# Summing the states of a selective scan: identity matmuls against PE transposes that add into one PSUM group

## The chip, the core and the metric

The kernel runs on one core of a Trainium2 chip. A core has TensorE (PE, matmuls, with its weight loads shown apart as PEld), VectorE (DVE), ScalarE (ACT), GpSimd (POOL) and SyncE (SP, which here issues transfers). PE writes its results to PSUM, and DVE and ACT read them from there; POOL works on the other memory, SBUF, alone. The metric is the device time of one execution in microseconds (us), the median of several runs, of the kernel before and the kernel after on the same chip.

## The reference

The program is four layers of a sequence model, each an attention-like block and a feed-forward block, on 2048 tokens of width 128 (8 sequences of 256 tokens in the layer that is changed). What is changed is the selective state space scan of the second layer, here cut to what matters. There are 256 inner channels and 16 states for each of them:

```python
xz = x @ W_in                                   # 128 -> 512
x_inner, z = jnp.split(xz, 2, axis=-1)
xc = silu(causal_conv4(x_inner) + conv_b)
x_ssm = xc @ W_xproj                            # 1 + 16 + 16 columns: delta, B, C
delta = softplus(delta_raw * w_dt + b_dt)
dA  = exp(delta[..., None] * A)                 # A = -exp(A_log)
dBx = delta[..., None] * Bm[:, :, None, :] * xc[..., None]
def step(h, (dA_t, dBx_t, c_t)):
    h = dA_t * h + dBx_t
    y = einsum('bdn,bn->bd', h, c_t)            # sum over the 16 states
y = y + xc * D_param
y = y * silu(z)
return y @ W_out                                # 256 -> 128
```

## The kernel before

All activations lie by channel: 128 channels on the partitions, tokens along the free dimension. A sequence of 256 tokens with 256 inner channels is a tile `[128, 2, 256]` (two halves `c` of the channels).

The stage that is touched is `local_mamba`. It interleaves three streams of work. `one_sequence` takes a sequence through two layers of local attention with their feed-forward blocks, up to four sequences at a time. Behind it `then` starts `mamba_sequence`, the state space of that sequence, with up to two of these under way. Beside the last one run loads of later weights, products of weight matrices (`fold`) and the routing of the first mixture of experts (`route1`).

In `mamba_sequence` (line 1216) the steps are: `xin` and the convolution into `xc`; `z` and `sz = silu(z)`, by channel (line 1242); `xps`, whose 33 rows go to memory and come back spread over all partitions as `bc`, with B and C of two states in each tile; `raw`, and from it `d` (delta) and `u = d * xc`. Then a loop over eight pairs of states, `m`:

- ACT makes `da = exp(d * A)`, four instructions of 128x255 (line 1295);
- DVE makes `hs = u * B` (line 1297), scans `hs` with `da` (line 1299), and multiplies by C (line 1300), each over 128x1024 elements: two states, two halves of channels, 256 tokens;
- PE adds the two states into the one PSUM tile `y` by two matmuls of 128x512 with the identity as weights (helper `mm`, line 863). Over the eight pairs 16 such matmuls form one PSUM group. In the profile an fp32 matmul is two instructions, so `y` has 256 of them for 128 matmuls.

After the loop DVE adds `xc * D_param` to `y` (line 1306, one instruction for each half), the product with `sz` follows on POOL (on DVE for the last sequence, line 1307), and `wout` takes the result to 128 channels. The residual `s` (line 1312), a layernorm and the router's logits close the sequence.

`route1` then works out for 14 of the 16 token tiles, and later for the last two, where each token goes (`put`, line 1512). `scatter` (line 1616) sends each tile of 128 tokens to its places by one indirect transfer that POOL issues, 16 in all. The first mixture of experts (`moe1`) reads `places` after all 16.

PSUM banks of the stage are shared by tag: two for the short-lived tiles (`M`: `xin`, `z`, `xps`, `raw`, `ln`, `wout` and others), two `Q`, one `A`, one `B`, one `Y` for `y`.

The order of instructions on each engine isn't the order of the program text. A planner (`_Order`) takes all instructions with their dependences, gives each a rank, its place in the text plus a correction from the table `BIAS` (by engine, tile name and stage), and a length from the table `LENGTHS`, plays the program through, and fixes the order that comes out for every engine. `STAY` is how much earlier in rank an instruction must be for PE or ACT to leave its present group (PE's shape of weights, ACT's function table). A change of these tables moves instructions in all stages.

Of the kernel before, what the change touches and what calls it, by code (L numbers as in the profile page):

```python
# [23 lines left out]
P = 128  # L24
# [285 lines left out]
class _Order:  # L310
# [12 lines left out]
    STAY = dict(PE=70, ACT=310)  # L323
    BIAS = {
        "ACT  1": 495, "ACT  3": -495, "ACT d 2": -1445, "ACT e 4": -700, "ACT e 6": 370, "ACT fh 4": -30, "ACT four 4": 630, "ACT four 5": -345,
        "ACT ge 2": 385, "ACT got 3": 50, "ACT got 5": 590, "ACT k 2": -275, "ACT kp 4": -40, "ACT lakq 2": -75, "ACT lavp 2": -95, "ACT lg 2": 620,
        "ACT lnrs 1": 225, "ACT lnrs 2": -280, "ACT lnsq 2": 40, "ACT ot 6": 75, "ACT ptsb 2": -740, "ACT qsq 2": -5, "ACT r 2": -70, "ACT rg 1": -590,
        "ACT rg 2": -320, "ACT rn 2": 55, "ACT rs 4": -50, "ACT rs 6": -25, "ACT s 6": -190, "ACT savp 2": -5, "ACT sg 3": 560, "ACT sh 5": -250,
        "ACT spl 1": -410, "ACT spt 1": -15, "ACT st 6": 460, "ACT v 2": 25, "ACT xc 2": -2725, "ACT xchunked 2": -400, "ACT xchunked 4": -390,
        "ACT xs 2": 10, "ACT xsq 4": -660, "DVE ab 4": 720, "DVE bt 3": -1225, "DVE bt 5": 190, "DVE centre 0": -205, "DVE d 2": -10,  # L330
        "DVE decaypart 4": -240, "DVE e 2": 50, "DVE four 5": 105, "DVE fs 4": 10, "DVE gate 2": -345, "DVE gate 5": -320, "DVE get 2": 180, "DVE get 4": 5,
        "DVE get 5": 850, "DVE got 4": -40, "DVE h 2": 5, "DVE h 5": -525, "DVE hs 2": 5, "DVE k 5": -680, "DVE lares 2": -200, "DVE lg 4": 665,
        "DVE nm 2": -135, "DVE nm 6": -95, "DVE oh 2": -285, "DVE oh 4": 2440, "DVE oh 5": -180, "DVE ptsb 2": 20, "DVE ptsb 6": -250, "DVE put 2": 190,
        "DVE put 4": 480, "DVE q 5": 470, "DVE q 6": 785, "DVE r 2": -120, "DVE rc 2": -270, "DVE rc 4": 175, "DVE route 2": -345, "DVE s 2": 20,
        "DVE s 5": -95, "DVE s 6": 1585, "DVE sares 2": 30, "DVE sel 4": -50, "DVE sg 3": -250, "DVE sm 4": 365, "DVE spt 1": 810, "DVE st 6": 150,
        "DVE sum 2": -705, "DVE t 5": 400, "DVE th 4": 650, "DVE u 2": 255, "DVE vec 2": 50, "DVE we 4": -30, "DVE wlocal 2": 1325, "DVE xc 2": -1830,
        "DVE xla 4": -580, "DVE xlf 4": 75, "DVE xlocal 2": -860, "DVE xmoe 6": 10, "DVE xpf 4": -10, "DVE xrglru 2": 205, "DVE xsa 4": 485, "DVE ys 3": 100,
        "DVE z 4": -190, "PE a 2": 50, "PE acc 5": 10, "PE b 2": 30, "PE bt 3": 1010, "PE bt 5": -580, "PE cum 2": 80, "PE cum 4": -1270, "PE fold 2": 105,
        "PE g 2": -700, "PE gate 1": -345, "PE gate 2": 345, "PE hps 4": -15, "PE kps 4": 95, "PE lg 2": 205, "PE lin 6": -1140, "PE ln 1": 355,
        "PE ln 2": -45, "PE o 6": -910, "PE out 4": -35, "PE pg 5": -20, "PE proj 5": 100, "PE proj 6": -570, "PE ps 4": -455, "PE pt 2": -25,  # L340
        "PE pt 4": -125, "PE pu 3": 2550, "PE pu 5": -720, "PE py 3": 740, "PE qkt 2": -1425, "PE raw 2": -1360, "PE rows 2": 585, "PE sc 2": -60,
        "PE sc 4": 30, "PE sc 6": -1215, "PE v 5": 470, "PE v 6": -20, "PE vps 2": 1025, "PE vps 4": -10, "PE wo 2": 60, "PE wo 6": -855, "PE wout 2": -95,
        "PE xps 2": -790, "PE y 2": 20, "PE z 2": 40, "PE zt 4": -20, "POOL biasrows 3": -595, "POOL e 4": 415, "POOL e 6": -305, "POOL got 5": 490,
        "POOL km 5": 665, "POOL mean 0": 635, "POOL one 0": 395, "POOL places 2": -70, "POOL places 5": -240, "POOL q 5": 50, "POOL q 6": -325,
        "POOL rest 4": -990, "POOL rg 1": -25, "POOL rows 4": 85, "POOL ss 2": -20, "POOL t 2": 595, "POOL u 2": 110, "POOL zero 0": -35,
        "POOL zeros 1": -385, "SP bc 2": 200, "SP cst 3": -455, "SP got 3": 535, "SP got 5": 505, "SP outdram 6": 275, "SP places 1": 1460,
        "SP rottable 0": 45, "SP routetables 0": 495, "SP rows 4": -370, "SP scales 2": 40, "SP vec 0": -1475, "SP wattn 2": 15, "SP wmoe 2": -150,
        "SP wmoe 4": -150, "SP wmoe 5": -100, "SP xs 2": -660,
    }
    LENGTHS = {  # L350
        "ACT  LoadActFuncSet  ": (1178, 1283), "ACT d Ln 128x512 128x512": (544, 649), "ACT da Exp 128x255 128x255": (403, 508),
        "ACT e Abs 128x256 128x256": (460, 565), "ACT e Exp 128x128 128x128": (422, 527), "ACT e Exp 128x256 128x256": (460, 565),
        "ACT e Exp 128x512 128x512": (526, 631), "ACT four Exp 128x2 128x2": (98, 203), "ACT got DMACopy 128x512 128x512": (451, 3502),
        "ACT h TensorCopy 64x255 64x255": (295, 400), "ACT k TensorCopy 128x512 128x512": (484, 589), "ACT lnrs Exp 128x256 128x256": (317, 422),
        "ACT lnsq Square 128x256 128x256": (278, 383), "ACT ot TensorCopy 128x512 128x512": (490, 595), "ACT qsq Square 128x512 128x512": (498, 603),
        "ACT r Relu 128x256 128x256": (462, 567), "ACT rg Exp 128x1020 128x1020": (1039, 1144), "ACT rg Ln 128x1024 128x1024": (949, 1054),
        "ACT rn Exp 128x16 128x16": (111, 216), "ACT rn Ln 128x16 128x16": (116, 221), "ACT rs Exp 128x2 128x2": (97, 202),
        "ACT rs Ln 128x2 128x2": (98, 203), "ACT sh Silu 128x512 128x512": (492, 597), "ACT xc Identity 128x256 128x256": (465, 570),
        "ACT xc Silu 128x512 128x512": (524, 629), "ACT xchunked TensorCopy 128x256 128x256": (260, 365), "ACT xmoe Identity 128x256 128x256": (404, 509),
        "ACT xs TensorCopy 33x256 33x256": (255, 360), "ACT xsq Square 128x128 128x128": (296, 401), "DVE biaspart TensorCopy 96x256 96x256": (198, 283),  # L360
        "DVE decay TensorScalarPtr 128x512 128x512": (516, 601), "DVE decaypart TensorCopy 128x512 128x512": (334, 419),
        "DVE four TensorScalarPtr 128x4 128x4": (74, 159), "DVE ge TensorScalarPtr 128x256 128x256": (384, 469),
        "DVE ge TensorScalarPtr 85x256 85x256": (368, 453), "DVE h TensorTensor 128x256 128x256": (317, 402),
        "DVE hs TensorScalarPtr 128x1024 128x1024": (2191, 2276), "DVE hs TensorTensor 128x1024 128x1024": (1123, 1208),
        "DVE mv BNStatsAggregate 128x2 128x6": (85, 170), "DVE nm TensorTensor 128x8 128x8": (67, 152), "DVE ptsb TensorCopy 128x512 128x512": (594, 679),
        "DVE rc Reciprocal 128x16 128x16": (158, 243), "DVE rc Reciprocal 128x4 128x4": (83, 168), "DVE rc Reciprocal 128x8 128x8": (109, 194),
        "DVE rg TensorScalarPtr 128x256 128x256": (580, 664), "DVE rottable TensorScalarPtr 128x256 128x256": (260, 345),
        "DVE s TensorScalarPtr 128x128 128x128": (253, 338), "DVE s TensorTensor 128x256 128x256": (324, 409), "DVE st BNStats 128x6 128x128": (197, 282),
        "DVE sum TensorReduce 128x32 128x448": (736, 821), "DVE t TensorScalarPtr 128x256 128x256": (385, 470),
        "DVE t TensorTensor 128x512 128x512": (595, 680), "DVE vec TensorTensor 128x1 128x1": (60, 145), "DVE vec TensorTensor 85x1 85x1": (59, 144),  # L370
        "DVE vs TensorCopy 128x512 128x512": (594, 679), "DVE wlocal TensorScalarPtr 128x682 128x682": (483, 568),
        "DVE x TensorScalarPtr 128x256 128x256": (369, 454), "DVE xc TensorScalarPtr 128x254 128x254": (384, 469),
        "DVE xla TensorScalarPtr 128x256 128x256": (429, 514), "DVE xlocal TensorTensor 128x256 128x256": (310, 395),
        "DVE xpf TensorScalarPtr 128x256 128x256": (577, 662), "DVE z TensorScalarPtr 128x128 128x128": (292, 377),
# [390 lines left out]
class _Kernel:  # L765
# [450 lines left out]
    def mamba_sequence(self, b, x, y, na, das, work, scan):  # L1216
# [22 lines left out]
        with ahead():  # L1239
            ps = self.psum("M", "z")  # L1240
            for c in range(2):
                self.mm(ps[:, c * S : (c + 1) * S], win[:, 256 + c * P : 256 + (c + 1) * P], x)
            sz = tile("sz", 2)
            nc.scalar.activation(flat(sz), ps, AF.Silu)
            self.exp_ln(nc.scalar.activation(xc, xc, AF.Silu))
# [1154 lines left out]
```

## Time and profile before

The profile is one execution; its own time stands beside the median.

| | |
|---|---|
| time, median of 3 runs | 1695.54 us (1694.59 to 1696.02) |
| time of the profiled execution | 1695.66 us |
| its span, first to last instruction | 1692.0 us |
| busy PE / DVE / ACT / POOL | 1442.4 / 1138.2 / 976.5 / 579.2 us |
| scans (line 1299), 64 instructions | 154.1 us, mean 2409 ns |
| products with B and with C (lines 1297, 1300), 64 each | 87.5 us each |
| matmuls into `y`, 256 instructions | 136.7 us, mean 647 ns |
| first and last matmul into `y` start at | 258.4 and 801.2 us |
| `D_param` step (line 1306), 16 instructions on DVE | median 471 ns |
| product with `sz` (line 1307) | 7 on POOL, median 1272 ns; 1 on DVE, 693 ns |

A busy share says how long an engine had an instruction under way. PE's instructions overlap, so the mean of one is longer than the time between two starts. An engine that is busy nearly all the time in a stretch sets its length; where none is, the idle time of the busiest and what ended it say what the others' speed is worth.

### The profile page before, as it was taken

Reading aid. Unit: us, or ns where it says so; the run is one execution under the profiler, and the core shown is the slowest. Engines: PE = TensorE matmul, PEld = TensorE weight load, DVE = VectorE, ACT = ScalarE, POOL = GpSimd, SP = SyncE. Lnnn points to the kernel's source line nnn. Section 1 sums busy time; section 2 is a strip of 40 time slices with the busy share of each in tenths; the row PEclk is TensorE's granted clock in tenths of the full one; section 3 lists DMA queues with packets and bytes.
Section 4 is the critical chain, followed back from the end, with each engine's and each line's share of the span. In section 5 each row is a group of like instructions: output and inputs, shape, how many; then the busy total and the mean of one; then the engine's idle time right before and its main releaser. Section 6 shows DMA issues by size and latency. Waiting matters only on the chain.

```text
span 1692.0 us, 28693 instructions
## 1 busy us (share of the span) xinstructions
PE 1442.4 (85%) x10858; PEld 932.5 (55%) x10858; DVE 1138.2 (67%) x2182; ACT 976.5 (58%) x2661; POOL 579.2 (34%) x535
## 2 busy tenths in 40 slices
PE   2688897979788877676679999999997998999997
PEld 1355553545454544343557776766674764566664
DVE  5755579898989898689354656566445332588885
ACT  3777887787877868644135554545443222366654
POOL 1344462616263423100331222221214004567573
PEclk7799999999999998899789999999997998999998
DMA  5000012121212213266310000000102121000000
GB/s 193 1 1 1 1 39 63 39 63 39 63 39 63 64 38 97 66 196 242 111 47 2 8 14 11 7 8 5 46 2 68 47 82 30 18 5 4 8 4 10
DMA packets 45113, 77.97 MB, mean 46 GB/s; under 512 B 5580, under 2 KB 21988, under 8 KB 43824
## 3 DMA queue, kind: packets, MB, share of 16 engines
q1 hardware_dynamic: 39648, 70.02, 13.8%
q0 software_dynamic: 3216, 5.07, 1.1%
q8 instruction: 85, 1.39, 0.3%
q10 hardware_dynamic: 2112, 1.05, 0.2%
q14 instruction: 52, 0.43, 0.1%
HBM read 66.87 MB, written 10.76 MB: 46 GB/s over the span
## 4 chain that ended last, share of the span: by engine, by line
PE 49%; DVE 23%; ACT 11%; issue 9%; POOL 5%; DMA 2%; another core or an unknown queue 0%; SPq 0%; ACTq 0%; DVEq 0%; POOLq 0%
PE vps L863 7%; PE kps L863 6%; PE sc L863 5%; PE out L863 4%; DVE hs L1299 3%; DVE hs L1300 3%; PE pu L863 3%; PE pg L863 3%; PE pt L974 3%; DVE hs L1297 2%; PE o L863 2%; ACT e L1146 2%; PE hps L863 2%; PE py L863 2%; PE acc L863 2%
## 5 line engine op out<-in xcount | busy, mean ns | idle before, releaser
L863 PE MATMUL y<-hs,ident 128*128 128x512 f32 x256 | 136.7, 647 | 30.2 <-DVE hs L1300 29.9
L1151 POOL TENSOR_TENSOR e<-e,rc 128x1024 f32<-128x1024 f32 x32 | 79.6, 2486 | 228.3 <-DVE rc L1150 227.6
L1299 DVE TENSOR_TENSOR_SCAN hs<-da,hs 128x1024 f32<-128x1024 f32 x64 | 154.1, 2409 | 0.1
L2250 ACT ACTIVATE e<-sc,nm 128x128 f32<-128x128 f32 (+1 forms) x256 | 105.1, 426 | 64.1 <-DVE nm L2245 55.2
L974 PE MATMUL pt<-ident,e 128*128 128x128 f32 x768 | 119.2, 281 | 18.0 <-POOL e L1151 12.4
L1295 ACT ACTIVATE da<-d,na 128x255 f32<-128x255 f32 x256 | 110.5, 508 | 22.5 <-DVE hs L1299 20.2
L1146 ACT ACTIVATE e<-sc,nm,rn 128x128 f32<-128x128 f32 x256 | 114.7, 468 | 10.9 <-DVE nm L1141 10.5
L974 PEld LDWEIGHTS pt<-ident,e 128*128 128x128 f32 x768 | 88.4, 143 | 56.3 <-issue 19.2
L2253 POOL TENSOR_TENSOR e<-e,rc 128x1024 f32<-128x1024 f32 x48 | 91.1, 1897 | 65.6 <-DVE rc L2252 65.5
L1829 POOL TENSOR_TENSOR e<-e,rc 128x512 f32<-128x512 f32 x32 | 33.9, 1059 | 226.1 <-DVE rc L1828 173.4
L1098 POOL TENSOR_TENSOR t<-t,t 128x512 f32<-128x512 f32 x64 | 84.1, 1316 | 61.1 <-DVE t L1085 56.0
L1651 POOL DMA_INDIRECT got<-ybuf,get x48 | 45.7, 952 | 169.0 <-DMA ybuf<-ys 87.6
L1804 ACT COPY kp<-kps 128x512 f32<-128x512 f32 x128 | 74.8, 585 | 48.5 <-PE kps L863 46.7
L1297 DVE TENSOR_TENSOR hs<-u,bc 128x1024 f32<-128x1024 f32 x64 | 87.5, 1384 | 6.2 <-POOL u L1284 5.5
L863 PEld LDWEIGHTS y<-hs,ident 128*128 128x128 f32 x256 | 47.5, 204 | 77.9 <-DVE hs L1300 47.5
L1300 DVE TENSOR_TENSOR hs<-hs,bc 128x1024 f32<-128x1024 f32 x64 | 87.5, 1369 | 0.0
L863 PE MATMUL qk<-w_local,h 128*128 128x512 f32 x128 | 71.1, 644 | 13.0 <-DVE t L1085 6.2
L976 DVE COPY ptsb<-pt 128x512 f32<-128x512 f32 x104 | 69.0, 677 | 17.0 <-PE pt L974 16.0
L1840 ACT COPY vs<-vps 128x512 f32<-128x512 f32 x64 | 37.4, 584 | 67.5 <-PE vps L863 56.8
L863 PE MATMUL vps<-sa_vp,x_lf 128*32 128x512 f32 x512 | 69.8, 594 | 0.0
L976 ACT COPY ptsb<-pt 128x512 f32<-128x512 f32 x88 | 51.4, 584 | 31.3 <-PE pt L974 30.7
L2245 DVE TENSOR_REDUCE nm<-sc 128x4 f32<-128x1024 f32 (+1 forms) x48 | 58.3, 1215 | 15.2 <-PE sc L863 14.6
(380 smaller groups left out, 3800.0 us busy)
## 6 DMA issues: line engine op xcount, KB each, us to landing
bc<-xs SPq DMA_DIRECT2D x128, 256.0 KB
w_moe<-in_e_dram SPq DMA_DIRECT2D x16, 768.0 KB
w_attn<-in_w_dram SPq DMA_DIRECT2D x4, 1024.0 KB
w_local<-in_w_dram SPq DMA_DIRECT2D x2, 1557.0 KB
places<-zeros SPq DMA_DIRECT2D x2, 1280.0 KB
got<-places SPq DMA_DIRECT2D x6, 256.0 KB
ybuf<-ys SPq DMA_DIRECT2D x8, 160.0 KB
x_in<-in_x_dram SPq DMA_DIRECT2D x1, 1024.0 KB
```

The source lines that it names most:

```text
L863: return self.nc.tensor.matmul(out, lhsT, rhs, start=start, stop=stop)
L974: self.last = self.nc.tensor.transpose(pt[:, j * P : (j + 1) * P], src[:, j * P : (j + 1) * P], self.ident)
L976: copy(sb.rearrange("p a b -> p (a b)"), pt)
L1098: nc.gpsimd.tensor_add(t1, t1, t2)
L1146: nc.scalar.activation(e[:, j, g, :], scs[:, j, g, :], AF.Exp, bias=nm[:, j, g : g + 1], scale=rq[:, j, g : g + 1], accum_out=sm[:, j, g : ...
L1151: nc.gpsimd.tensor_tensor(e, e, rc.unsqueeze(3).to_broadcast([P, 2, 4, P]), ALU.mult)
L1295: nc.scalar.activation(da[:, n, c, 1:S], d[:, c, 1:S], AF.Exp, scale=na[:, i : i + 1])
L1297: nc.vector.tensor_tensor(hs, u.unsqueeze(1).to_broadcast(shp), bn, ALU.mult)
L1299: nc.vector.tensor_tensor_scan(line(hs), line(da), line(hs), 0.0, ALU.mult, ALU.add)
L1300: nc.vector.tensor_tensor(hs, hs, cn, ALU.mult)
L2250: nc.scalar.activation(e[:, i, :], sc[:, i, :], AF.Exp, bias=nm[:, i : i + 1], accum_out=sm[:, i : i + 1])
L2253: nc.gpsimd.tensor_tensor(e, e, rc.unsqueeze(2).to_broadcast([P, n, keys]), ALU.mult)
```

## The change

The sum over states is made in the other layout, by token. For each state, four PE transposes of 128x128 (two halves of channels, two tiles of 128 tokens) write to the PSUM tile `y`, now `[128 tokens, 2 tiles, 256 channels]`, and add into one PSUM group: 8 transposes for each pair of states in place of 2 matmuls of 128x512. The data is now the weights, and the identity is the moving operand. `xc * D_param` is made beforehand, on POOL, in place in `xc`, and joins the same group by four more transposes. `sz` is made by token too (the operands of the `z` matmul change sides; 2 matmuls of 128x256 as before). One DVE product of 128x512 gates `y` by `sz`; four transposes into a PSUM tile `yg` of the `M` banks and one ACT copy of 128x512 bring the result back to channels for `wout`.

With it come new tables for the planner: `STAY`, all of `BIAS`, and most of `LENGTHS` are replaced (three lines of each stand below).

```diff
-    STAY = dict(PE=70, ACT=310)
+    STAY = dict(PE=110, ACT=480)
     BIAS = {
-        "ACT  1": 495, "ACT  3": -495, "ACT d 2": -1445, "ACT e 4": -700, "ACT e 6": 370, "ACT fh 4": -30, "ACT four 4": 630, "ACT four 5": -345,
...
+        "ACT  1": 600, "ACT bt 5": 610, "ACT da 2": -25, "ACT e 2": 5, "ACT e 4": 5, "ACT fh 4": -15, "ACT four 4": -50, "ACT four 5": 80, "ACT ge 2": 385,
...
     LENGTHS = {
-        "PE xps Matmult 33x256 128x256": (447, 602), "PE y Matmult 128x512 128x512": (1107, 1218), "PE z Matmult 128x256 128x256": (438, 599),
...
@@ mamba_sequence
-            for c in range(2):
-                self.mm(ps[:, c * S : (c + 1) * S], win[:, 256 + c * P : 256 + (c + 1) * P], x)
+            for t in range(2):
+                self.mm(ps[:, t * S : (t + 1) * S], x[:, t * P : (t + 1) * P], win[:, 256:512])
...
             eng.tensor_mul(u, d, xc)
+            nc.gpsimd.tensor_tensor(xc, xc, self.v("dpar", 0, 2).unsqueeze(2).to_broadcast([P, 2, S]), ALU.mult)
         yield 3.0
-        yp = self.psum("Y", "y")
+        yp = self.psum("Y", "y").rearrange("p (t c d) -> p t c d", t=2, c=2)
+
+        def gathered(src, first, last):
+            for c in range(2):
+                for t in range(2):
+                    self.nc.tensor.matmul(
+                        yp[:, t, c, :], src[:, c, t * P : (t + 1) * P], self.ident, start=first and c + t == 0, stop=last and c + t == 2, is_transpose=True
+                    )
+
...
             for n in range(2):
-                self.mm(yp, self.ident, flat(hs[:, n]), m == 0 and n == 0, m == 7 and n == 1)
+                gathered(hs[:, n], m == 0 and n == 0, False)
             yield 2.3
-        yg = tile("t")
+        gathered(xc, False, True)
+        nc.vector.tensor_tensor(flat(sz), yp.rearrange("p t c d -> p (t c d)"), flat(sz), ALU.mult)
+        ps = self.psum("M", "yg")
         for c in range(2):
-            nc.vector.scalar_tensor_tensor(yg[:, c, :], xc[:, c, :], self.v("dpar", c), yp[:, c * S : (c + 1) * S], ALU.mult, ALU.add)
-        eng.tensor_mul(yg, yg, sz)
+            for t in range(2):
+                nc.tensor.transpose(ps[:, c * S + t * P : c * S + (t + 1) * P], sz[:, t, c * P : (c + 1) * P], self.ident)
+        nc.scalar.copy(flat(sz), ps)
         ps = self.psum("M", "wout")[:, 0:S]
         for c in range(2):
-            self.mm(ps, wout[:, c, :], yg[:, c, :], c == 0, c == 1)
+            self.mm(ps, wout[:, c, :], sz[:, c, :], c == 0, c == 1)
```

In the order that the planner fixes, the sequences, the pairs of states and the layers of local attention follow each other on DVE much as before: 246 DVE instructions of other kinds stand ahead of the first product with C, where there were 247, and 604 ahead of the 61st, where there were 609. Near the end of the stage two things move. The conversion `put` for the first 14 token tiles, which stood behind the scan of the last pair of states of the last sequence, now stands ahead of the scan of its fourth pair. And the conversions and sums of the gate (`L1535` before) stand between the last pairs rather than behind them. The orders of all other stages differ in many places as well.

## The prediction, made before the changed kernel ran

> **What bounds the kernel now.** I read the busy table by stage first. The stage of the change runs from the first scan (about 240 us) to the last product (803 us):
>
> ```profile
> 240.00:803.00 563.00, 452.34 (x2474) 261.31 (x2474) 496.68 (x576) 413.11 (x1035) 197.66 (x168) 0.95 0.29 82
> 803.00:830.00 27.00, 10.10 (x43) 7.67 (x43) 7.13 (x29) 4.45 (x9) 14.44 (x17) 0.56 0.25 66
> 830.00:1300.00 470.00, 440.56 (x4801) 323.80 (x4800) 261.63 (x844) 215.61 (x509) 105.08 (x114) 0.96 0.08 22
> 1300.00:1692.00 392.00, 363.57 (x2459) 236.12 (x2458) 230.90 (x501) 172.67 (x677) 171.53 (x122) 0.97 0.09 26
> ```
>
> The columns are the stretch, its length, busy PE, PEld, DVE, ACT and POOL, PE's granted clock, transfers. In the first row DVE is busy 496.7 of 563 us (88%), PE 452.3 (80%), ACT 413.1: DVE sets the pace, and its 66 us of idle time are what others can win back. After 830 us PE is busy 93 to 94% with work that the change doesn't touch.
>
> Second, what ended DVE's idle time in that stretch (waits, engine DVE):
>
> ```profile
> DVE t L1277 <- ACT e L1275: 18.6, 6, 5.5
> DVE s L1312 <- PE wout L863: 6.8, 3, 3.8
> DVE ss L1079 <- ACT qsq L1078: 6.8, 9, 1.5
> DVE ge L1204 <- PE a L863: 4.1, 6, 2.5
> DVE x L1179 <- PE wo L863: 3.0, 3, 1.0
> DVE ptsb L976 <- PE pt L974: 2.9, 2, 2.1
> DVE t L1083 <- PE qkt L1103: 2.5, 3, 1.3
> DVE nm L1140 <- PE sc L863: 2.0, 2, 1.6
> ```
>
> Here the numbers are the total, how often, and the longest. The rows that PE ends sum to 21.3 us. The row `ss <- qsq`, 6.8 us, is PE's at one remove, since `qsq` reads `qk`. No row has a scan waiting for PE: the matmuls into `y` come behind DVE.
>
> Third, the groups of instructions and the chain of waits, for the price of the two ways of summing:
>
> ```profile
> L863 PE MATMUL y<-hs,ident 128*128 128x512 f32 x256 | 136.7, 647 | 30.2 <-DVE hs L1300 29.9
> L976 ACT COPY ptsb<-pt 128x512 f32<-128x512 f32 x88 | 51.4, 584 | 31.3 <-PE pt L974 30.7
> 292.30 1.72 PE y L863 x4
> 831.15 0.44 PE bt L1643 x4
> ```
>
> In the chain, one pair of states (four instructions into `y`) costs 1.72 us, 0.43 each. Four transposes of 128x128 cost 0.44 us, 0.11 each, with their weight loads behind them.
>
> Fourth, the timeline at the end of the stage, DVE and POOL:
>
> ```profile
> 798.45 0.14 DVE L1512 CAST put<-route 128x14 int32<-128x14 f32 x1
> 799.48 1.32 POOL L1616 DMA_INDIRECT places<-x_chunked,put  x1 [50.34 <-DVE get L1523]
> 801.11 0.99 POOL L1616 DMA_INDIRECT places<-x_chunked,put  x1 [0.30 <-issue]
> 813.43 0.18 DVE L1512 CAST put<-route 128x2 int32<-128x2 f32 x1
> 819.24 0.97 POOL L1616 DMA_INDIRECT places<-x_chunked,put  x1 [0.30 <-issue]
> 821.44 1.49 SPq L1636 DMA_DIRECT2D got<-places  x3
> ```
>
> POOL had waited 50 us for `put` of the first 14 tiles. From 799.5 to 820.2 us its 16 scatters, one each 1.28 us, are what the next stage waits for.
>
> **The change part by part.** The sum is made against the profiled execution: 1695.66 us, 0.12 us above the median.
>
> *DVE.* Removed: 16 instructions of line 1306 at 0.471 us (7.5 us) and the last sequence's own product, 0.69 us. Added: 8 gates of 128x512 with one operand in PSUM; the nearest row, line 1083 of that form, has 0.68 us: 5.4 us. DVE has 2.8 us less in a stage that it paces, and I count it whole. For the gate, the other PSUM row of this size (the copy at line 976, mean 0.677) gives the same; a row without PSUM (line 1307, 0.693) gives 2.7.
>
> *PE.* Removed: 256 instructions at 0.43 us, 110 us. Added: 512 transposes at 0.11 us, 56 us; and 8 times 8 for `xc` and the way back, 7 us. PE has 47 us less of 452. That is not on the path: `y` is only 10.7 us of the chain between 240 and 803 us, of 85 us that PE has on it. What it is worth is a shorter queue ahead of the other matmuls, so a part of 21.3 + 6.8 = 28.1 us of DVE's idle time. Lower bound 0 (those waits may all be latencies), upper bound 28.1. The saving on the chain itself gives 10.7 x 47/110 = 4.6 us directly; PE's share of the stage falls by a tenth, and a queue falls by more than its load does. I take 8 us, between the direct 4.6 and half of the bound.
>
> *The way back.* From the last product of a sequence to `wout`, before: 4 instructions into `y` and their drain (799.85 to 801.83 in the timeline), two halves of line 1306, the product with `sz`, in all 3.8 us for the last sequence. After: 12 transposes at 0.11 and one drain of 0.16 (four take 0.60 from the first start), the gate 0.68, four transposes 0.60, one ACT copy 0.58, four hand-overs of about 0.06: 3.6 us. I count 0. The other sequences lose POOL's 1.27 us product on that path and gain the copy and the transposes, again 0. ACT's 8 copies (4.7 us) are hidden by its idle time, 150 us here; queued behind them on ACT are `da` and the exponentials of local attention, and the scan waits for `da` 0.1 us in all. With that cover gone they cost 4.7 us.
>
> *POOL.* Seven products with `sz` (1.27 us) go, eight of `xc` with `D_param` come, priced by the same row: 1.3 us more, in 365 us of idle time. They stand behind `u`, and only the last four transposes of the group need them. No step waits.
>
> *z by token.* The same 2 matmuls of 128x256: 0.
>
> *The moved scatters.* `put` of 14 tiles moves from behind the last scan (798.45) to ahead of the fourth pair's scan, which in the profile starts at 778.36. The first 14 scatters then take 14 x 1.28 = 18 us from about 779 us, beside the scans. After the last `put` (813.43) only two remain: 1.0 us to POOL's start (as 798.45 to 799.48), 1.32 + 0.30 + 0.97, and 1.2 us to the transfers, 818.2 in place of 821.4 us: 3.2 us gained. What was hidden behind POOL is late next, namely the last sequence's own chain. Moved gate sums cost nothing there: before, DVE did them while PE filled `y`.
>
> *The new order elsewhere.* Nothing in the other stages is added or removed. The table loads of ACT are 72 for 74. From 830 us on PE is full, and an order can change only the 6 to 7% of its idle time. I take 0 and keep 8 us to both sides, a tenth of the idle time of the busiest engine outside the stage (PE's: 64 us before 240 us, 29 and 28 us after 830), rounded up.
>
> Sum: 2.8 + 8 + 3.2 = 14.0, **1682 us**.
>
> [...] In the profile PE's granted clock is 0.98 from 240 to 640 us, where matmuls of all kinds fill it, and 0.83 and 0.87 in these two, where it is less busy:
>
> ```profile
> 640.00:680.00 40.00, 30.41 (x140) 16.58 (x138) 37.71 (x37) 30.74 (x83) 10.69 (x7) 0.83 0.35 90
> 680.00:720.00 40.00, 25.50 (x97) 13.27 (x98) 27.25 (x31) 26.20 (x51) 6.72 (x7) 0.87 0.25 67
> ```
>
> [...]
>
> **The rivals.** *PE's relief is hidden* (DVE is full, its waits are latencies): only 2.8 + 3.2 remain, 1689.7 us. For it: no scan waits for PE. Against it: 21.3 us of idle time that PE's results end.
>
> *The hand-over gives it back.* `yg` takes one of two `M` banks and crosses to ACT, so `wout` comes later; DVE's 6.8 us at `s <- wout` double: 1689.7 + 6.8 = 1696.5 us, no change. For it: ACT is 73% busy, and its queue is in order. Against it: POOL made the same detour before.
>
> *The clock falls* (slower). Place: all of 240 to 803 us. Price: the 85 - 11 = 74 us of other PE work on the chain stretch with 0.95/clock. At 0.70, midway between 0.83 above and the 0.56 of the idle stretch after 803 us, that is 26 us, so 1682 + 26 = 1708 us. It decides from the clock at which 74 x (0.95/clock - 1) = 14, that is 0.80; the two stretches above are nearly there already. Against it: PE stays 72% busy, (452 - 47) of 563 us, and local attention's matmuls stand between the transposes until 640 us.
>
> **How the numbers follow.** My forecast 0.46; relief hidden 0.20; given back 0.11; clock 0.23. The likeliest case alone reaches from 1668 (PE's relief at two thirds of its bound, 3 us from the order elsewhere) to 1690. For 8 in 10 the range is 1664 to 1704: below, 26 of the 28.1 us of idle time instead of 8; above, a clock of 0.73 (22 us by the same formula). A measurement of this kernel tells 0.2%, 3.4 us, from no change: faster 0.66 (the first two), same 0.11, slower 0.23.
>
> **What would show it.** Right: four transposes into `y` in 0.44 us; DVE's busy time in the stage 3 us lower and its idle time 60 us or less; the last PE-ended waits shorter; two scatters alone after the last `put`; the stages from 830 us on of the same length within 4 us each. Wrong: a clock under 0.8 between 240 and 803 us; more idle time ahead of `s` at `wout`; a stage without an edit that is 8 us or more off, which would mean that the new order, and not the sum, decides.

## The result and the profile after

The changed kernel took 1706.5 us, the median of 19 runs (1694.64 to 1713.39), beside 1695.54 us for the kernel before in as many (1693.65 to 1698.13). The ratio is 1.0055, with a 95% interval of 1.0042 to 1.0068: 9 us slower (the medians differ by 11), where 14 us faster was forecast. The runs of the changed kernel spread over 19 us, those of before over 4.5. The profiled execution is one of the quicker ones: 1701.73 us, span 1699.7 us.

First the busy table by stage of the changed kernel (columns as before: stretch, length, PE, PEld, DVE, ACT, POOL, clock, transfers); the last three rows are the chunked attention, the second mixture of experts and the rest:

```profile
240.00:803.00 563.00, 431.09 (x2786) 295.57 (x2784) 498.56 (x566) 419.25 (x1047) 224.81 (x177) 0.90 0.28 79
640.00:812.00 172.00, 109.76 (x630) 81.14 (x628) 143.31 (x146) 93.82 (x213) 41.98 (x29) 0.74 0.44 144
826.40:1270.80 444.40, 425.91 (x4659) 309.85 (x4660) 237.85 (x713) 207.25 (x473) 91.15 (x100) 0.97 0.08 24
1270.80:1470.30 199.50, 179.13 (x899) 115.63 (x891) 73.55 (x239) 49.86 (x109) 51.54 (x52) 0.94 0.18 51
1470.30:1699.70 229.40, 206.08 (x1733) 137.76 (x1731) 181.93 (x397) 135.62 (x606) 134.63 (x87) 0.98 0.02 7
```

and the same three later stages in the kernel before:

```profile
821.40:1263.70 442.30, 419.50 (x4623) 310.86 (x4627) 239.31 (x710) 204.33 (x470) 91.24 (x100) 0.97 0.08 24
1263.70:1460.30 196.60, 178.06 (x933) 118.17 (x925) 72.82 (x239) 51.05 (x113) 48.62 (x50) 0.92 0.18 51
1460.30:1692.00 231.70, 211.53 (x1735) 135.66 (x1733) 181.38 (x400) 134.25 (x606) 137.53 (x89) 0.98 0.02 7
```

Against the first row before, PE has 21 us less work in the stage (452.3 to 431.1), not 47. DVE has 1.9 us more (496.7 to 498.6), not 2.8 less, and POOL 27 us more. The clock is 0.90 for 0.95, and 0.74 in the stretch after local attention, where the kernel before has 0.90 (640 to 803 us). The chunked attention, in which no instruction was edited, has 6.4 us more of PE's busy time (419.5 to 425.9), the last row 5.5 us less; over the three later rows it is 2.0 us more.

Second, what ended DVE's idle time from 240 to 805 us (total, how often, longest):

```profile
DVE t L1277 <- ACT e L1275: 11.3, 6, 3.3
DVE s L1324 <- PE wout L863: 10.2, 6, 5.7
DVE x_mamba L918 <- ACT ln_rs L917: 8.6, 3, 4.3
DVE ss L1079 <- ACT qsq L1078: 7.7, 9, 1.9
DVE ptsb L976 <- PE pt L974: 4.7, 4, 2.5
```

The wait for ACT's `e` is 7 us shorter. Of the ones that PE ends, which were to become shorter, `s` is 3.4 us and `ptsb` 1.8 us longer, and `ss`, PE's at one remove, 0.9; `ge` (4.1 to 1.0), `x <- wo` (3.0 to 0.4) and `t <- qkt` (2.5 to 1.4) did become shorter. In all PE ends 25.5 us of DVE's idle time here, for 21.7 before.

Third, the groups of the sum and of the products with B:

```profile
L1292 PE MATMUL y<-ident,hs 128*128 128x128 f32 x512 | 90.6, 323 | 41.5 <-DVE hs L1309 41.1
L1306 DVE TENSOR_TENSOR hs<-u,bc 128x1024 f32<-128x1024 f32 x64 | 94.6, 1491 | 5.6 <-POOL u L1284 4.8
```

The transposes come to 0.177 us each over the stage, where 0.11 was priced. The product with B, which is the same instruction as before, has a mean of 1491 ns in place of 1384.

Fourth, the timeline at the end of the stage, DVE, PE, POOL and SP's queue:

```profile
785.17 0.17 DVE L1524 CAST put<-route 128x14 int32<-128x14 f32 x1
786.21 2.29 POOL L1628 DMA_INDIRECT places<-x_chunked,put  x1 [19.85 <-ACT sa_vp L1756]
788.81 1.87 POOL L1628 DMA_INDIRECT places<-x_chunked,put  x1 [0.30 <-issue]
807.87 1.97 PE L1292 MATMUL y<-ident,hs 128*128 128x128 f32 x8 [1.49 <-DVE hs L1309]
822.00 0.16 DVE L1524 CAST put<-route 128x2 int32<-128x2 f32 x1
824.18 0.97 POOL L1628 DMA_INDIRECT places<-x_chunked,put  x1 [0.30 <-issue]
826.38 1.49 SPq L1648 DMA_DIRECT2D got<-places  x3
```

The scatters did move: the first 14 run beside the last pairs, and from the last `put` to the read of `places` it is 4.4 us (822.00 to 826.38) where it was 8.0. But the last `put` itself comes 8.6 us later than before (813.43), so that `got` starts 5.0 us later.

So one profile shows a stage 5 us longer and later stages 3 us longer. It can't say which of the three things in the change did it: the sum, the order inside the stage, or the order of the stages behind it. For the experiments an order was written into a kernel, instruction by instruction, for each engine; two kernels whose instructions are the same but for the sum could so be given each other's order.

One thing must be known for reading them. The runs were made in five lots. In the first two the kernel before took 1674.5 and 1674.4 us, in the other three 1695.8, 1697.1 and 1695.3. Each ratio is to the kernel before in the same lot.

### The profile page after: what moved, and what is told of

Its sections match the earlier page's. It is cut to its first block, busy times and chain, and to the rows that moved or that the text cites. A ratio compares the mean times of both kernels' runs of the same rounds, so it can differ in the third digit from the quotient of the medians.

```text
span 1699.7 us, 29309 instructions
## 1 busy us (share of the span) xinstructions
PE 1424.6 (84%) x11178; PEld 969.2 (57%) x11178; DVE 1139.9 (67%) x2173; ACT 982.0 (58%) x2667; POOL 598.4 (35%) x536
## 4 chain that ended last, share of the span: by engine, by line
PE 53%; DVE 25%; ACT 9%; issue 7%; POOL 4%; DMA 1%; another core or an unknown queue 0%; ACTq 0%; SPq 0%; DVEq 0%; POOLq 0%
PE vps L863 7%; PE kps L863 6%; PE sc L863 6%; DVE hs L1308 5%; PE out L863 4%; PE pt L974 3%; PE pu L863 3%; PE pg L863 3%; PE o L863 3%; DVE hs L1306 3%; DVE hs L1309 3%; ACT e L1146 2%; PE py L863 2%; PE hps L863 2%; PE acc L863 2%
## 5 line engine op out<-in xcount | busy, mean ns | idle before, releaser
L974 PE MATMUL pt<-ident,e 128*128 128x128 f32 x768 | 114.6, 280 | 14.5 <-POOL e L1151 6.9
L1292 PE MATMUL y<-ident,hs 128*128 128x128 f32 x512 | 90.6, 323 | 41.5 <-DVE hs L1309 41.1
L1098 POOL TENSOR_TENSOR t<-t,t 128x512 f32<-128x512 f32 x64 | 88.4, 1385 | 61.7 <-DVE t L1085 48.7
L1292 PEld LDWEIGHTS y<-ident,hs 128*128 128x128 f32 x512 | 71.5, 167 | 65.9 <-DVE hs L1309 57.6
L1306 DVE TENSOR_TENSOR hs<-u,bc 128x1024 f32<-128x1024 f32 x64 | 94.6, 1491 | 5.6 <-POOL u L1284 4.8
L1309 DVE TENSOR_TENSOR hs<-hs,bc 128x1024 f32<-128x1024 f32 x64 | 83.6, 1308 | 0.0
L863 PE MATMUL vps<-sa_vp,x_lf 128*32 128x512 f32 x512 | 78.0, 594 | 0.0
L863 PE MATMUL vps<-la_vp,x_moe 128*32 128x512 f32 x512 | 72.3, 595 | 0.6 <-DVE vs L1852 0.6
```

The lines of the kernel that those rows point to most:

```text
L863: return self.nc.tensor.matmul(out, lhsT, rhs, start=start, stop=stop)
L974: self.last = self.nc.tensor.transpose(pt[:, j * P : (j + 1) * P], src[:, j * P : (j + 1) * P], self.ident)
L1098: nc.gpsimd.tensor_add(t1, t1, t2)
L1292: self.nc.tensor.matmul(yp[:, t, c, :], src[:, c, t * P : (t + 1) * P], self.ident, start=first and c + t == 0, stop=last and c + t == 2, ...
L1306: nc.vector.tensor_tensor(hs, u.unsqueeze(1).to_broadcast(shp), bn, ALU.mult)
L1309: nc.vector.tensor_tensor(hs, hs, cn, ALU.mult)
```

## The experiments

### Transposes against matmuls of the same shape; tables exchanged (first lot)

```diff
-  yp[:, t, c, :], src[...], self.ident, ..., is_transpose=True
+  yp[:, t, c, :], src[...], self.ident, ..., is_transpose=False      # e1_mm_all
+  yp[:, t, c, :], src[...], self.ident, ..., is_transpose=b < 5      # e2_mm_late
```

> The changed kernel with the same order and layout, but the sum over states made by ordinary fp32 matmuls with the identity (data as weights) in place of transposes: about 50 us more of PE work, and work of another kind. Clock theory (transposes do not hold PE's clock up): the granted clock from 640 to 812 us, 0.74 in the changed kernel, comes back to about 0.90; the median falls to 1690 to 1699 us and the runs spread by 5 us instead of 19. Order theory (the new tables are what costs): the clock is no matter, PE is 50 us fuller, the median stays at 1705 us or rises to 1715.

> As the first, but ordinary matmuls only for the last three of the eight sequences; the first five keep transposes. Clock theory: the 6 us that the changed kernel is ahead of the one before at the fifth sequence are kept, and the loss after 570 us goes: 1686 to 1695 us, narrow spread. Order theory: 1704 to 1712 us.

Measured: 1703.22 us, ratio 1.0173 (1.0150 to 1.0196), and 1696.10 us, 1.0116 (1.0100 to 1.0132). The clock between 640 and 812 us was 0.88 and 0.84 in place of 0.74; over the whole profiled execution it was 0.945 and 0.936, for 0.930 in the changed kernel. Matmuls brought the clock back and yet no time: as ordinary fp32 matmuls these instructions kept PE busy for longer (126 us in that stretch in the first of the two, for 110), and neither kernel beats the changed one (1.0103 in the next lot, with the same time for the kernel before).

In the next two the tables alone are exchanged: `STAY`, `BIAS` and `LENGTHS` of the changed kernel in the kernel before, and the other way round.

```diff
-    STAY = dict(PE=70, ACT=310)       # e3: the kernel before; e4 the reverse
+    STAY = dict(PE=110, ACT=480)      # with all of BIAS and LENGTHS
```

> The kernel before, with the planner's tables of the changed one (order alone changes). Clock theory: 1691 to 1699 us with the narrow spread of the kernel before. Order theory: 1702 to 1708 us.

> The changed kernel with the planner's tables of the kernel before. Clock theory: a clock near 0.75 from 640 us on, a wide spread (10 us or more), 1698 to 1712 us. Order theory: 1682 to 1695 us, narrow spread.

Measured: 1740.55 us, ratio 1.0400 (1.0383 to 1.0417), and 1726.82 us, 1.0311 (1.0297 to 1.0325). None of the four times lies where one of the two theories had it; both were reckoned from a kernel before of 1695 us, which here takes 1674. With either sum the planner's tables of the other give an order that is 3 to 4% worse. This tells nothing about the sum, only that an order can weigh more than it.

### The two sums in each other's order (second lot)

```diff
-        order, _ = self.plan()
+        order = the instructions of each engine, sorted by their places in the other kernel's order
```

> The changed kernel itself, as a control on the chip of the three other runs. Both theories: 1.004 to 1.007 times the kernel before, a spread of 10 us or more, a granted clock of about 0.75 from 640 to 812 us.

> The changed kernel with every instruction that both kernels have at its place in the order of the kernel before; the new ones stand where those that they replace stood. Order theory (the new tables cost, the new sum does not): 0.988 to 0.999 of the kernel before. Clock theory (transposes let the clock sink): 1.004 to 1.015, with a clock near 0.75 from 640 us on and a wide spread.

> The kernel before with every common instruction at its place in the order of the changed kernel. Order theory: as slow as the changed kernel or slower, 1.005 to 1.02, though the clock is up (0.88 or more from 640 us on). Clock theory: 0.993 to 1.003, narrow spread.

> The kernel before, for its trace on the same chip: within 0.3% of its other runs there, the clock 0.90 from 640 to 803 us.

Measured: the changed kernel 1691.59 us, ratio 1.0103 (1.0088 to 1.0119); the new sum in before's order 1697.24, 1.0148 (1.0123 to 1.0174); **the old sum in the new order 1691.27, 1.0092 (1.0076 to 1.0108)**. The kernel before in its new order is as slow as the changed kernel, without any edit to the sum. Where that goes, by the start of `got`: the stage ends at 824.6 us (before), 825.6 (changed) and 827.7 (old sum, new order), but from there to the end it takes 849.8, 863.8 and 863.1 us. With the old order there (new sum) it is 849.4. So in this lot the order of the later stages costs 13 to 14 us with either sum.

The new sum in before's order is a miss for the order theory (0.988 to 0.999): the whole loss of 1.0148 lies in the stage, which ends at 845.4 us, 21 us later than with the old sum in that order. The new sum needs its own order in the stage, so the two don't simply add up.

What the later stages lose is for the most part PE's busy time. The sums over the three stages behind `got`, with the same 7281 PE instructions, first the kernel before, then the changed one:

```profile
sum 849.30, PE 799.74 PEld 560.06 DVE 494.10 ACT 389.10 POOL 276.57; mean PE 266.58 PEld 186.69 DVE 164.70 ACT 129.70 POOL 92.19
sum 863.80, PE 809.59 PEld 563.00 DVE 493.59 ACT 392.92 POOL 276.73; mean PE 269.86 PEld 187.67 DVE 164.53 ACT 130.97 POOL 92.24
```

Of the 14 us, 10 are PE's busy time. The groups of PE in the chunked attention, from 870 to 1250 us, again first the kernel before, then the changed one:

```profile
L863 PE MATMUL vps<-la_vp,x_moe 128*32 128x512 f32 x512 | 66.6, 594 | 0.2 <-DVE vs L1840 0.2
L863 PE MATMUL out<-vs,ptsb 128*32 128x128 f32 x912 | 37.7, 274 | 0.0
L863 PE MATMUL sc<-kp,x_lf 128*32 128x128 f32 x512 | 24.7, 275 | 0.0
```

```profile
L863 PE MATMUL vps<-la_vp,x_moe 128*32 128x512 f32 x512 | 71.7, 595 | 0.0
L863 PE MATMUL out<-vs,ptsb 128*32 128x128 f32 x908 | 43.9, 274 | 0.0
L863 PE MATMUL sc<-kp,x_lf 128*32 128x128 f32 x512 | 27.6, 275 | 0.0
```

The mean time of one instruction is the same (the profile models where a matmul ends), and so is their number, within the records that are missing; the busy time of a group is 3 to 6 us longer. Busy time counts overlapping instructions once. Counted in the two traces, the start of one `vps` follows the last by 0.094 us inside an unbroken run in both, but the 512 come in 50 runs before and in 62 in the new order; all PE instructions behind `got` come in 1280 and 1378, with either sum. So the instructions of a group overlap less with each other. That more broken runs are the reason of the 10 us fits, but was not tried by itself.

### The order of the later stages alone (third lot)

Two kernels change over at the first mixture of experts: the changed kernel with before's order from there on (e7), and the kernel before with the changed kernel's order from there on (e8).

```diff
-        order = the kernel's own
+        order = the kernel's own up to the end of the stage, the other kernel's behind it
```

> The changed kernel with its own order through the state-space stage, and from the first mixture of experts on the order of the kernel before (the instructions there are the same in both). Theory (the order of the later stages costs 14 us, whichever sum is used, and the new sum itself costs the stage 1 us): the time is that of before + 1 us, ratio 0.998 to 1.003, and from the read of the places (got) to the end it takes what before takes, within 3 us. Rival (the new sum or its low clock leaves something behind that slows the later stages): the loss after got stays, ratio 1.008 to 1.011. The reasoning on record in the prediction, that an order outside the stage changes nothing by itself, expects the same ratio as for the changed kernel, 1.010.

> The kernel before with its own order through the state-space stage, and from the first mixture of experts on the order of the changed kernel. No instruction is changed. Theory (the order of the later stages): 14 us more than before, ratio 1.007 to 1.010, all of it after got: some 10 us in the chunked attention and 5 in the second mixture of experts, with longer mean times of the 128x32-column matmuls (vps 0.130 to 0.140 us of busy time each) and not more idle time. Rival (the loss comes with the new sum): ratio 1.000. A second rival (the loss in the old-sum kernel with the new order came from the stage): also 1.000 here.

Measured: 1692.83 us, ratio **0.9979** (0.9963 to 0.9994), and 1700.28 us, **1.0036** (1.0022 to 1.0050). In the second no instruction is changed and none before `got` moved; it is slower all the same. The size is smaller than the 14 us expected: here, as in the first profile, the kernel before needs 20 us more than in the first two lots, 14 of them in the chunked attention (442.3 against 428.4 us), where the new order has less to lose. The traces of the runs with so long a kernel before say the same: from `got` to the end the three with the new order there take 873.3 to 873.6 us (the changed kernel in the first profile and in the fourth lot, and this second kernel), the nine with the old one 866.8 to 870.6. That is 3 to 7 us.

### A mixed sum (third lot)

In the changed kernel the clock was 0.95 from 240 to 640 us and 0.74 from 640 to 812, behind local attention. So sequences 0 to 4 use transposes and 5 to 7 the old sum. Of the edit the choice of the sum is shown; the other steps of the change, POOL's product among them, go with it.

```diff
+            new = b < 5
...
+                if new:
+                    gathered(hs[:, n], m == 0 and n == 0, False)
+                else:
+                    self.mm(yf, self.ident, flat(hs[:, n]), m == 0 and n == 0, m == 7 and n == 1)
```

> Sequences 0 to 4 by transposes, 5 to 7 by identity matmuls, in the changed kernel's order through the stage and in before's order from the first mixture of experts on. Theory (the transposes relieve PE while local attention fills it, and lose by the clock once it does not): the stage is 6 us ahead at sequence 4, as the changed kernel was, and then takes the 258 us from there to got that the old sum took in the new order, so got comes 3 us earlier than before: ratio 0.997 to 1.000, the granted clock from 640 us to the end of the stage 0.84 to 0.88. Rival (the loss in sequences 5 to 7 is the new order's alone): as the changed kernel's stage, ratio 1.000 to 1.003.

> As the kernel with the mixed sum, but the order goes over from the changed kernel's to before's gradually between the planner's 500 and 620 us, so that sequences 5 to 7 run in the order of before with the sum of before. Theory: 6 us ahead at sequence 4, then the 254 us that before takes from there to got: 5 to 8 us less than before, ratio 0.995 to 0.997. Rival (an order between two that were worked out for other programs fits neither): 5 us or more above before, ratio over 1.003.

Measured: 1689.96 us, ratio **0.9970** (0.9959 to 0.9982), and 1706.02 us, 1.0066 (1.0045 to 1.0087). The first is as expected. The second is a miss, and the rival stood there: in the stretch where the two orders cross, it is 86 us from the start of one sequence's delta to the next one's (`t <- e`, 566.6 to 652.6 us) where it was 73 in the first (563.7 to 636.6). Here an order between two good ones was a worse one.

### The sum alone, in one order (fourth lot)

Four kernels side by side: the changed kernel (f1); the same with before's order later (f2, the same kernel as e7, which had 0.9979 in the third lot); the old sum in that second order (f3); and the mixed sum with sequence 5 by transposes as well (f4).

```diff
-            new = b < 5
+            new = b < 6      # f4
```

> The changed kernel again, so that the next three have it beside them. Ratio 1.0055 as on the first chip, or 1.010 as on the second.

> The changed kernel with before's order from the first mixture of experts on, beside the changed kernel on one chip. Theory (the later order is the largest part of the loss): 8 to 14 us less than the changed kernel, ratio to before 0.997 to 1.002. Rival (that order costs 3 to 6 us, as the profiles on the first chip say, and the rest was the difference of chips): ratio to before 1.002 to 1.005 where the changed kernel has 1.0055, and 1.007 where it has 1.010.

> The old sum in the changed kernel's order through the stage, and before's order from the first mixture of experts on: against the run with the new sum in the same order everywhere it shows the sum alone. Theory (relief of PE early and a low clock late cancel): within 3 us of that run, ratio to before 1.000 to 1.003. Rival (the new sum is a gain of the size that the prediction gave to DVE and PE, 10.8 us, and only the order hid it): 8 us or more above that run.

> As the mixed sum, but sequence 5 by transposes too; 6 and 7 by identity matmuls. Theory (transposes lose from the point where local attention no longer fills PE, about 640 us, where sequence 5 begins): 1 to 2 us above what the mixed sum had, ratio 0.998 to 0.999. Rival (only the very last sequences lose): 1 to 2 us below, ratio 0.995 to 0.996.

Measured:

| kernel | us | ratio to before (95%) |
|---|---|---|
| f1: new sum, new order | 1703.96 | 1.0039 (1.0022 to 1.0057) |
| f2: new sum, new order in the stage only | 1696.86 | 0.9994 (0.9980 to 1.0007) |
| f3: old sum, new order in the stage only | 1696.09 | 0.9998 (0.9988 to 1.0008) |
| f4: as f2, old sum from sequence 6 on | 1692.00 | 0.9979 (0.9960 to 0.9997) |

From f1 to f2 the order of the later stages alone is 7.1 us, as much as the changed kernel loses in this lot; that is less than the theory expected (8 to 14) and more than its rival (3 to 6), and the two traces put 3.4 us of it behind `got`. The mean granted clock of the runs is the same, 0.928. From f2 to f3 the sum alone, in the new order of the stage, is 0.8 us, nothing that can be told from zero, and both stand where before stands. f4 lies at the theory's edge (0.998 to 0.999 expected, 0.9979 measured), but its interval holds the rival's 0.996 too: whether sequence 5 still gains from transposes stays open.

The waits of DVE in f3, which has the old sum with all its 256 instructions, from 240 to 805 us:

```profile
DVE t L1396 <- ACT e L1394: 11.5, 6, 3.4
DVE s L1431 <- PE wout L982: 10.4, 6, 3.8
DVE x_mamba L1037 <- ACT ln_rs L1036: 8.8, 3, 4.3
DVE ss L1198 <- ACT qsq L1197: 7.9, 12, 1.9
DVE ptsb L1095 <- PE pt L1093: 5.1, 5, 2.5
DVE x L1330 <- PE w L982: 4.3, 5, 1.0
```

The first five are those of the changed kernel within 0.4 us each (11.3, 10.2, 8.6, 7.7, 4.7), and of f2 too. The sixth isn't; f2 has

```profile
DVE x L1331 <- PE w L983: 1.3, 1, 1.3
```

In all PE ends 31 us of DVE's idle time in f3 and 28 in f2, by one trace each. So the new sum does shorten the waits, by some 3 us; the rest of them belong to the order, not to how full PE is.

The rows of the clock in the stretch behind local attention, first f2, then f3:

```profile
640.00:812.00 172.00, 110.55 (x638) 81.86 (x637) 143.46 (x146) 95.98 (x219) 42.50 (x28) 0.75 0.45 147
```

```profile
640.00:805.00 165.00, 115.21 (x523) 63.13 (x522) 140.25 (x148) 95.32 (x217) 39.25 (x26) 0.87 0.45 151
```

In the same order, 0.75 with transposes and 0.87 with matmuls. PE is busy for 64% of the stretch in f2 and for 70% in f3, but the busy share alone doesn't give the clock: in the row of 680 to 720 us of the kernel before, which the prediction shows, PE is busy for 64% too, and its clock is 0.87; in the same 40 us of the changed kernel it is busy for 70%, and the clock is 0.73. So the clock was lower with transposes at a like busy share; by what mechanism was not shown.

### POOL's new product (fifth lot)

f2 and f3 have the same order, and yet DVE is busy for 1141.8 us in f2 and 1133.4 in f3, though the edit takes 2.2 us off DVE there (line 1425 and the last product, 7.0 + 0.7, for eight gates, 5.5). The difference lies in the products with B. The two timelines where sequence 1 begins, first f2, then f3 (DVE and POOL):

```profile
329.61 4.60 DVE L1426 TENSOR_TENSOR hs<-u,bc 128x1024 f32<-128x1024 f32 x2
329.88 1.03 POOL L1405 TENSOR_TENSOR xc<-xc,vec 128x512 f32<-128x512 f32 x1
331.14 4.20 POOL L1218 TENSOR_TENSOR t<-t,t 128x512 f32<-128x512 f32 x2
```

```profile
331.91 3.60 DVE L1416 TENSOR_TENSOR hs<-u,bc 128x1024 f32<-128x1024 f32 x2
332.44 4.20 POOL L1217 TENSOR_TENSOR t<-t,t 128x512 f32<-128x512 f32 x2
```

Two products with B take 4.60 us with POOL's product of `xc` and `D_param` beside them and 3.60 without: DVE is longer by 1.00 us, and POOL's instruction is 1.03 long. (Both times hold other work of POOL, `t <- t,t`, which f2 and f3 share.) So DVE lost here about the length of POOL's instruction; by what mechanism was not shown. The last two kernels take that product off POOL; g1 is f2, g2 is the mixed sum of the third lot.

```diff
-            nc.gpsimd.tensor_tensor(xc, xc, self.v("dpar", 0, 2).unsqueeze(2).to_broadcast([P, 2, S]), ALU.mult)
+            for c in range(2):
+                nc.scalar.activation(xc[:, c, :], xc[:, c, :], AF.Identity, scale=self.v("dpar", c))
```

> The new sum in the changed kernel's order through the stage and before's order later (as f2), with the product of xc and D_param made by ACT, two instructions of 128x256 for each sequence some 6 us later, in place of one on POOL. Theory (that product, beside the first products with B of a sequence, stretches them by 1 us each): the products with B fall from 96.9 to 90 us or less, DVE's busy time by 5 us or more, and the time by 2 to 6 us against f2, ratio to before 0.996 to 0.998. Rival (they are stretched by POOL's other work, whichever comes beside them): they stay above 95 us, ratio 0.998 to 1.001.

> The mixed sum (sequences 0 to 4 by transposes, 0.997 before) with the product of xc and D_param on ACT for these five sequences. Theory: 2 to 4 us less than the mixed sum had, ratio 0.994 to 0.996. Rival: as the mixed sum, 0.996 to 0.998; above 0.998 if ACT's queue pays for it.

Measured: 1691.84 us, ratio 0.9980 (0.9971 to 0.9989), and 1687.44 us, **0.9961** (0.9947 to 0.9975). The group of the products with B, in f2, f3 and g1:

```profile
L1426 DVE TENSOR_TENSOR hs<-u,bc 128x1024 f32<-128x1024 f32 x64 | 96.9, 1528 | 5.1 <-POOL u L1404 4.8
```

```profile
L1416 DVE TENSOR_TENSOR hs<-u,bc 128x1024 f32<-128x1024 f32 x64 | 88.3, 1394 | 6.3 <-POOL u L1403 4.7 <-PE y L982 1.4
```

```profile
L1427 DVE TENSOR_TENSOR hs<-u,bc 128x1024 f32<-128x1024 f32 x64 | 89.2, 1407 | 5.8 <-POOL u L1404 5.0 <-PE y L1413 0.4
```

Without POOL's product 7.7 of the 8.6 us are gone, and DVE's busy time in the program falls from 1141.8 to 1133.0 us. That this product made them longer is shown. What it is worth in time is not: by the ratios 0.0014, 2.4 us, against f2, with intervals that overlap (f2 0.9980 to 1.0007), and nothing against the same kernel in the third lot (e7, 0.9979). g1 has the low clock still, 0.74 from 640 to 812 us, and is faster than before all the same.

g2 has the lowest ratio: mixed sum, `D_param` on ACT, the new order in the stage, the old one behind it; 0.4% faster than before where the changed kernel is 0.55% slower. Its ratio lies between the theory (0.994 to 0.996) and the rival (0.996 to 0.998), and its interval overlaps that of the mixed sum with POOL's product (0.9959 to 0.9982), so what ACT's product adds there stays open.

## Why the prediction was wrong

**The step that failed, and turned the sign:** "The new order elsewhere. [...] From 830 us on PE is full, and an order can change only the 6 to 7% of its idle time. I take 0 and keep 8 us to both sides". PE's busy time isn't fixed by its instructions: behind `got` it is 799.7 us in one order and 809.6 in the other, in the second lot. In time the later order is +7.1 us (f1 against f2), 0.36% (e8) and 14 us in the second lot, where the chunked attention is 9.8 us longer (428.4 to 438.2), the very sign that the prediction named for being wrong. The bound of 8 us was kept in the range, but taken from the wrong quantity, PE's idle time. That each later stage was within 4 us in the first profile (2.1, 2.9 and -2.3 us), which the prediction named as a sign of being right, was no such sign: together they are 2.7 us, and the profiled run was 4.8 us below the median.

That step explains the sign. The size also needs the 14.0 us that were to be gained in the stage: the new sum with the old order behind `got` is level with the kernel before in one lot and 3 us faster in another (f2 0.9994, e7 0.9979). Term by term:

**PE, 8 us:** some 3 us of shorter waits, and no time in the end. The reading "a shorter queue ahead of the other matmuls, so a part of [...] DVE's idle time" was too large: with the old sum in the same order (f3) PE ends 31 us of DVE's idle time, with the new one (f2) 28, and the longest rows are the same. What those 3 us would be worth without POOL's product beside them isn't shown. PE's share of the stage did fall, by 21 us of busy time and not 47; eight transposes, priced at 0.88 us, take 1.97 where PE had been idle before them (807.87 in the timeline) and 1.10 between other matmuls (at 260.91).

**DVE, -2.8 us:** the edit's own instructions were priced rightly (a gate has 0.686 us, 0.68 priced; f2 against f3 -2.2). The term was lost to the line "POOL [...] No step waits". POOL's product needs 1.67 us in the mean (1.03 to 2.08) for the 1.27 priced, which is hidden; but the products with B beside it grew by 8.6 us of DVE's time (f2 against f3), and without it by 0.9 (g1). The cost of an instruction on POOL was looked for among its readers, and lies with DVE, whose products with B ran beside it (4.60 us for two, 3.60 without it).

**The moved scatters, -3.2 us:** the price was right: from the last `put` to `got` it is 3.6 us less. What was "hidden behind POOL", the last sequence's own chain, was late by more: the last `put` comes 8.6 us later.

**The way back, 0:** for the last sequence it is 5.0 us from the last product to `wout` (807.82 to 812.81), for 3.84 before; the twelve transposes take 2.8 us there (807.87 to 810.69) where 1.5 was counted. But the old sum in the new order is no quicker: from the last product to `s` f3 takes 6.0 us (804.38 to 810.41) and the changed kernel 6.2 (807.82 to 813.98).

**The rival of the clock** gave 1708 us, close to the 1706.5 measured by luck: the lower clock is real, 0.74 behind local attention, 0.75 against 0.87 in one order, but it isn't what made the kernel slower. With the same low clock and only the later order put back the loss is gone (f2, g1), and matmuls that held the clock at 0.84 to 0.88 were no faster (e1, e2). It was placed over the whole stage at 0.70; there the clock was 0.90, and from 240 to 640 us 0.95. That PE's other work takes longer by 0.95/clock was an estimate, and no run shows it by itself. It may have a part in the spread: of the 19 runs of the changed kernel the two shortest have a clock of 0.930 and 0.931 and the longest 0.919, but whether the clock is the cause isn't shown, and with as low a clock the spread is 13 us in f2 and 8 in g1 (7 in f3, with the old sum). Giving up transposes for the last two sequences took 4.9 us off f2 (f4, with intervals that overlap), though two of POOL's products go with them, so that this isn't the clock alone either. **The hand-over rival** had the sign of the wait at `wout` right (6.8 to 10.2 us), but f3, which has no hand-over, has 10.4.

## What to carry to other kernels

Where an edit comes with a new order for the whole program, they are two changes: give the old code the new order, and the new code the old order where nothing was edited, before pricing the edit by the total. An instruction moved to an idle engine is priced by what runs beside it, too: POOL was 65% idle, and its product cost DVE 8 us of busy time. And less work on an engine was worth here only the waits that were queues behind that work: 3 of 31 us.

## What was not expected of the hardware

- The same 7281 instructions kept PE busy for 799.7 us in one order and for 809.6 in another, and for 809.1 in the first of these orders in the first profile.
- The same kernel before took 1674.4 us in two lots of runs and 1695.3 to 1697.1 in three and for the result, with a spread of 3 to 9 us in a lot. The difference lies in the chunked attention (428.4 and 442.3 us) and the second mixture of experts (189.1 and 196.6), with the same instructions in the same order. One group has the largest part of it: the matmuls `out <- vs,ptsb` keep PE busy for 37.7 us from 870 to 1250 us in the second lot, and in the first profile for 41.8 with 4.8 us of idle time ahead of them. It isn't the chip, since the second and the fifth lot ran on the same one. What differs between the lots stays open.
- POOL's scatters of 0.97 to 1.32 us took 1.35 to 2.29 us beside DVE's scans and products.
